# Moving mask clears, counts and first list steps in a sparse two-layer graph attention kernel

## The chip, the core and the metric

The kernel runs on one core of a Trainium2 chip, as one program and one launch. The metric is the device time in microseconds from the start to the end of the program: three runs of the kernel before gave 1828.33, 1829.27 and 1834.35 us, so its median is 1829.27 us.

The engines are named as the profile names them: PE is TensorE's matmul, PEld its weight load, DVE is VectorE, ACT is ScalarE, POOL is GpSimd, SP is SyncE, which here only issues DMAs.

## The reference

Two graph attention layers over 3327 nodes with 1024 features, each with a residual and a layer norm. The adjacency is 0 or 1, symmetric, with some 16 neighbours per node and its diagonal set. Layer 0 has 8 heads of 128, layer 1 has one head of 1024.

```python
# layer 0
h = (x @ W).reshape(C, H, D)
alpha_src = einsum('hcd,hd->hc', h_heads, a_src)
alpha_dst = einsum('hcd,hd->hc', h_heads, a_dst)
e = alpha_src[:, :, None] + alpha_dst[:, None, :]
e = where(e >= 0, e, 0.2 * e)
e = where(adj[None] == 0, -inf, e)
out = einsum('hij,hjd->hid', softmax(e), h_heads)
x = layernorm(x + out)
# layer 1: h = x @ W; the same with one head, a relu, a residual and a layer norm
```

## The kernel before

Nodes are cut into NT = 26 tiles of 128 (P). The kernel has two stages. The first one, "projection with list work", projects each tile of x with the weights of layer 0, stores the rows of h in device memory, and beside it turns each tile's dense adjacency rows (a mask of 128 x 3328 bytes) into lists of neighbours. The second stage, `sparse`, gathers the listed rows of h with indirect DMAs, weighs and sums them, and does layer 1 in the same manner. A third part, `by_pairs`, is for dense graphs and isn't entered with this input. The change touches only the first stage.

In that stage nothing is scheduled by the compiler: `manual_schedule` (L510) keeps the order in which the Python code issues instructions, on every engine. Each engine runs its own instructions in that order and waits with semaphores for what the others make.

The projection of a tile t has three column cuts c of 347, 347 and 346 columns. `flip(t, g)` (L533) transposes half of x's tile on PE into the one PSUM bank "T" and copies it out on ACT (L199). `project(t, c)` (L538) does the eight matmuls over k into one of two banks "A". `keep(t, c)` (L549) copies the result out on ACT (L561); for c = 2 it also copies the scores (L556) and makes `factors`, small exponentials on ACT and four small instructions on POOL (L329 to L333). After the third cut the rows go out with a DMA on SP (L564).

The list work of a tile has these steps:

- `words` (L335): POOL clears the tile's own diagonal block in the mask with an affine_select (L342); ACT passes twice over the mask to count each row's neighbours in two halves (L346, into `junk`) and makes `deg_b` (L348); DVE folds eight mask bytes into one word (L353, `wd`, three instructions). `count(t)` (L566) calls it and then issues the load of the mask two tiles ahead on POOL's DMA queue (`load_mask`, L524). There are three mask buffers.
- `ends` (L359): a tiny PE matmul of `deg_b` with a triangle (L362) makes running sums over the rows; ACT copies them (L367) and 13 small POOL instructions make places of them (L369 to L382).
- `ends2` (L384): the same for what overflows: PE (L387), ACT (L388), six POOL instructions (L389 to L395).
- `keys` and `columns` (L397, L406), two calls each: DVE picks each row's largest words, then its columns (L308, L310).
- `ways` (L421), three ACT instructions; `places` (L431), DVE (L435 to L441); `spread` (L443), four ACT instructions (L447, `mvg`).
- `give` (L451), five times: PE matmuls that move the lists to their places (L459, L466). `take` (L470): ACT copies the result (L478 to L485) and SP stores a part. `sources` (L488): DVE makes the indices of the gathers (L493 to L507).

The generator `listing` (L572) puts these into rounds. Round t has, in order: four steps with `give` of tile t and `keys` or `columns` of tile t+1, with `ends(t+3)` in the second and `ends2(t+3)` in the fourth; one step with the last two `give`, `take(t)`, `ways(t+1)` and `count(t+4)`; one with `sources(t)`; one with `places(t+1)`; one with `spread(t+1)`. That is eight steps; round -1 has no tile t and is shorter.

`pace` (L608) advances the generator: it is called after every second k of a paced `project`, and keeps the number of steps done at a share of the paces so far. `slots` holds the paces counted and the paces in all; `done` the steps done.

Before the main loop (L854) the first tiles are issued by hand (L779 to L853): `count(0)`, two steps of the generator, cuts of tiles 2 and 0, `ends` of tile 0, `count(1)`, two more steps, and so on, as the diff shows. In the main loop iteration t projects cuts 0 and 1 of tile t and cut 2 of tile t+1 and flips tile t+2. From t = 13 (NTH) on, `sums_so_far` (L617) joins: it gathers rows of h that are already stored (L629, POOL), makes weights (DVE, L637 to L650) and sums them on PE (L659); each pace advances it by one step as well.

Of the kernel before, what the change touches and what calls it, by code (L numbers as in the profile page):

```python
# [14 lines left out]
OP = mybir.AluOpType  # L15
# [4 lines left out]
P = 128  # L20
# [6 lines left out]
def kernel(  # L27
# [28 lines left out]
    nc = tc.nc  # L56
    N, D = x.shape
    H, DH = a0_src.shape
    NT = (N + P - 1) // P
# [254 lines left out]
    class Edges:  # L314
# [10 lines left out]
        def factors(self):  # L325
# [6 lines left out]
            nc.gpsimd.tensor_copy(mv[:, 1, :], r[:, 1, :])  # L332
            nc.gpsimd.tensor_tensor(mv[:, 2, :], r[:, 1, :], mv[:, 1, :], OP.subtract)  # L333

        def words(self, ad, junk):  # L335

            sbuf, ph, t = self.ph.sbuf, self.ph, self.t  # L340
            own = ad[:, t * P : (t + 1) * P].bitcast(mybir.dt.int8)
            nc.gpsimd.affine_select(  # L342
                out=own, in_=own, pattern=[[1, P]], compare_op=OP.not_equal, fill=0.0, base=0, channel_multiplier=-1
            )
            for n in range(2):
                nc.scalar.activation(junk, ad[:, n * THR : (n + 1) * THR], AF.Copy, accum_out=self.d[:, n : n + 1])  # L346
            self.deg_b = sbuf("deg_b", [P, 2], 4, dt=BF16)
            nc.scalar.activation(self.deg_b, self.d, AF.Copy)  # L348
            w = ad.bitcast(I32)
            for n in range(3):  # L350
                m = WD >> n
                half = sbuf(f"wd{n}", [P, m], 4 if n == 2 else 1, dt=I32)
                nc.vector.scalar_tensor_tensor(  # L353
                    half, w[:, m:], 1 << n, w[:, :m], op0=OP.logical_shift_left, op1=OP.bitwise_or
                )
                w = half
            self.bytes = w.bitcast(U8)
# [152 lines left out]
    with ExitStack() as own, tc.manual_schedule():  # L510
        ph = Phase(own, "proj", {"A": 2, "T": 1})
# [4 lines left out]
        xts, xT, ads, hts, accs = {}, {}, {}, {}, {}  # L516
        lists = [Edges(ph, t) for t in range(NT)]

        def load_x(t):
            if t < NT:  # L520
                xts[t] = ph.sbuf("x", [P, D], 2)
                load_rows(xts[t], x, t)
# [10 lines left out]
        def flip(t, g, who=None):  # L533
            if g == 0:
                xT[t] = ph.sbuf("xT", [P, KT, P], 2) if t else part.sbuf("z", [P, KT, P], 1, "xT")
            (who or ph).turned(xT[t], xts[t] if g == 0 else xts.pop(t), g)

        def project(t, c, paced=True, between=None):  # L538

            acc = accs[t, c] = bank("A", [P, CUTS0[c + 1] - CUTS0[c]], "mm")  # L540
            for k in range(KT):
                nc.tensor.matmul(  # L542
                    acc, xT[t][:, k, :], wt[:, k, CUTS0[c] : CUTS0[c + 1]], start=k == 0, stop=k == KT - 1
                )
                if k == 3 and between:
                    between()
                if paced and k % 2 == 1:
                    pace()

        def keep(t, c):  # L550
            if t not in hts:
                hts[t] = ph.sbuf("ht", [P, HW0], 3)
            ht, acc, c0 = hts[t], accs.pop((t, c)), CUTS0[c]
            m = min(CUTS0[c + 1], D) - c0
            if c == 2:
                nc.scalar.activation(sd0[:, t].rearrange("p a h -> p (a h)"), acc[:, m:], AF.Copy)  # L556
                lists[t].factors()
                nc.scalar.activation(ht[:, D : D + H], acc[:, m + H :], AF.Exp)
                nc.scalar.activation(ht[:, D + H :], acc[:, m + H :], AF.Exp, scale=SLOPE)
                scored.add(t)  # L560
            nc.scalar.activation(ht[:, c0 : c0 + m], acc[:, :m], AF.Copy)  # L561
            kept[t] = kept.get(t, 0) + 1
            if kept[t] == 3:
                nc.sync.dma_start(h0_d[t * P : (t + 1) * P, :HW0], hts.pop(t))  # L564

        def count(t):  # L566
            if t < NT:
                lists[t].words(ads.pop(t), junk)
                if t:
                    load_mask(t + 2)  # L570

        def listing():  # L572

            for t in range(-1, NT):
                old, new = lists[t] if t >= 0 else None, lists[t + 1] if t + 1 < NT else None
                for s in range(4):
                    if old and s:
                        old.give(s - 1)
                    if new:
                        (new.keys, new.columns)[s // 2](s % 2)  # L580
                    if s == 1 and 2 < t + 3 < NT:
                        lists[t + 3].ends(tri_b)
                    if s == 3 and 2 < t + 3 < NT:
                        lists[t + 3].ends2(all_b)
                    yield
                if old:
                    old.give(EB - 1)
                    old.give(EB)
                    old.take()
                if new:  # L590
                    new.ways()
                count(t + 4)
                yield
                if old:
                    old.sources()
                    yield
                while new and t + 1 not in scored:
                    yield
                if new:
                    new.places()  # L600
                    yield
                    new.spread()
                    yield

        scored, kept, soon = set(), {}, []
        steps, slots, done = listing(), [0, 0], [0]

        def pace():  # L608
# [202 lines left out]
        for g in range(NG):  # L811
            nc.vector.memset(tri[g * GT : (g + 1) * GT, g * GT : (g + 1) * GT], 1.0)
        nc.gpsimd.affine_select(
            out=tri, in_=tri, pattern=[[1, P]], compare_op=OP.is_ge, fill=0.0, base=0, channel_multiplier=-1
# [8 lines left out]
        )  # L823
        all_b = pool.tile([P, P], BF16, bufs=1, name="all_b")
        nc.vector.tensor_copy(all_b, tri)
        count(0)
        for _ in range(2):
            next(steps)
# [8 lines left out]
        project(1, 2, False)  # L837
        keep(1, 2)
        lists[0].ends2(all_b)
        lists[1].ends(tri_b)  # L840
        flip(3, 0)
        load_x(5)
        count(2)

        done[0], slots[:] = 4, [9, (NT - 3) * 12 + 13]
        project(2, 2, True, lambda: flip(3, 1))
        keep(2, 2)
        flip(4, 0)
        lists[1].ends2(all_b)
        lists[2].ends(tri_b)  # L850
        project(3, 2, True, lambda: flip(4, 1))
        keep(3, 2)
        lists[2].ends2(all_b)  # L853
        for t in range(3, NT):  # L854
            load_x(t + 3)
            if 4 <= t < 4 + KT:
                nc.sync.dma_start(wt1[:, t - 4, :], w1[(t - 4) * P : (t - 3) * P, :])
            if t == 12:
                n, own_a = NT - 1, pool.tile([P, NT], I32, bufs=1, name="own")
                nc.vector.memset(own_a[:, n:], 0)  # L860
                step, m = adj.ap[0][0] + 1, rows(n)
                nc.sync.dma_start(
                    own_a[:, :n], bass.AP(tensor=adj.tensor, offset=adj.offset, ap=[[step, P], [P * step, n]])
                )
                nc.sync.dma_start(
                    own_a[:m, n:], bass.AP(tensor=adj.tensor, offset=adj.offset + n * P * step, ap=[[step, m], [1, 1]])
                )
            if t == 11:
                ph.iota([P, P], [[1, P]], "io_t", base=1, dst=io_t)
                same = ident[: NG * H, : NG * H].rearrange("p (g h) -> p g h", g=NG)  # L870
                met = meets.rearrange("p (g t) -> p g t", g=NG)
                nc.vector.tensor_reduce(met[:, :, 0], same, AX.X, OP.max)
                nc.vector.tensor_copy(met[:, :, 1:], met[:, :, :1].to_broadcast([NG * H, NG, GT - 1]))
                nc.vector.tensor_reduce(heads, same.rearrange("p g h -> p h g"), AX.X, OP.max)
            if t == 16:
                nc.gpsimd.tensor_copy(loop, own_a)
            if t in (9, 10):
                table, w = (h0_d, HW0) if t == 9 else (y_d, HW)
                blank = pool.tile([P, 1, HP - w], F32, bufs=1, name=f"blank{t}")
                nc.gpsimd.memset(blank, 0.0)  # L880
                nc.sync.dma_start(
                    table[:, w:].rearrange("(t p) w -> p t w", p=P), blank.to_broadcast([P, NT, HP - w])
                )
            if t == NTH:
                soon.append(sums_so_far())
            for c in (0, 1):
                project(t, c)
                keep(t, c)
            if t + 2 < NT:
                flip(t + 2, 0)  # L890
            if t + 1 < NT:
                project(t + 1, 2)
                keep(t + 1, 2)
            if t + 2 < NT:
                flip(t + 2, 1)
# [624 lines left out]
```

## Time and profile before

One execution was profiled. It took 1945.79 us, with a span of 1944.1 us from the first to the last instruction; the three timed runs lie at 1828.33 to 1834.35 us.

| what | value |
|---|---|
| median of the timed runs | 1829.27 us |
| profiled execution | 1945.79 us |
| its span | 1944.1 us |
| PE busy | 1633.7 us, 84% |
| DVE busy | 1184.5 us, 61% |
| POOL busy | 1092.2 us, 56% |
| ACT busy | 573.4 us, 29% |
| one clear of a mask block (L342, POOL, x26) | 294 ns |
| one count pass (L346, ACT, x52) | 1591 ns |
| first fold of words (L353, DVE, x26) | 591 ns |
| DVE waiting for the clear (L353 <- L342), 0 to 600 us | 57.0 us, 13 times |
| ACT waiting for the clear (L346 <- L342), 0 to 600 us | 14.8 us, 5 times |

The busy shares are means over both stages. The first stage ends near 570 us of the span; what happens there has to be read from that stretch. A matmul's busy time in the profile is modelled, since matmuls overlap. In the profile's lines the number after the name of an engine is the line of the kernel; "<-" names what ended a wait.

### The profile page before, as it was taken

What the parts mean: (1) busy time and instruction counts of PE and PEld (TensorE: products, weight loads), DVE (VectorE), ACT (ScalarE), POOL (GpSimd) and SP (SyncE); (2) the same over time, 40 slices, a digit from 0 to 9 for tenths busy, and PEclk for the clock granted to TensorE, in tenths of its full rate; (3) what the DMA queues carried; (4) which work ended last, traced back from release to release, by engine and by line L of the source; (5) the groups of instructions that cost most, each with busy time, mean ns of one, the idle gap of its engine ahead of it and who ended that gap; (6) DMA issues with size and microseconds to landing.
All of it is one profiled execution on the core that took longest, in us unless ns stands there. A gap on an engine that the chain in (4) does not pass through costs nothing.

```text
span 1944.1 us, 35431 instructions
## 1 busy us (share of the span) xinstructions
PE 1633.7 (84%) x13168; PEld 919.9 (47%) x13168; DVE 1184.5 (61%) x3261; ACT 573.4 (29%) x1565; POOL 1092.2 (56%) x1580
## 2 busy tenths in 40 slices
PE   8699989989994777777777665798989999899988
PEld 5466556655563554554455442243434434333433
DVE  6699988777765776777777774243444344434342
ACT  5656554444321222222222121022122221222121
POOL 4433346656555666666666555565656666565640
PEclk9899999999996878888878877899999999999999
DMA  6555779887779999999999998899999999899980
GB/s 178 91 130 114 144 152 293 255 249 238 247 271 349 381 391 393 383 393 371 402 386 386 374 313 301 310 374 340 346 350 369 335 394 342 331 362 340 325 302 33
DMA packets 183364, 585.16 MB, mean 301 GB/s; under 512 B 36168, under 2 KB 42824, under 8 KB 183182
## 3 DMA queue, kind: packets, MB, share of 16 engines
q0 software_dynamic: 131056, 457.74, 68.4%
q1 hardware_dynamic: 52126, 125.06, 17.2%
q8 instruction: 107, 1.75, 0.4%
q14 instruction: 75, 0.61, 0.1%
HBM read 586.09 MB, written 51.22 MB: 328 GB/s over the span
## 4 chain that ended last, share of the span: by engine, by line
PE 43%; issue 10%; DVE 6%; ACT 4%; DMA 4%; POOL 1%; another core or an unknown queue 0%; DVEq 0%; ACTq 0%; POOLq 0%
PE mm L1267 17%; PE acc L1235 13%; PE acc L1129 8%; PE acc L1110 2%; DMA src<-h_d,idx 2%; PE tr L196 1%; ACT L1193 1%; PE acc L1118 1%; DVE e L1098 1%; ACT own L1076 1%; DMA near<-h_d,idx 1%; DVE pr L982 1%; DVE st L217 1%; ACT L220 1%; DMA src<-y_d,idx 1%
## 5 line engine op out<-in xcount | busy, mean ns | idle before, releaser
L542 PE MATMUL mm<-wt,xT 128*128 128x347 f32 (+1 forms) x1248 | 416.6, 475 | 6.8 <-ACT ht L561 3.3
L1267 PE MATMUL mm<-wt,xT 128*128 128x512 f32 x832 | 395.5, 613 | 2.6 <-issue 2.3
L1017 POOL DMA_INDIRECT src<-y_d,idx x248 | 249.1, 1005 | 166.8 <-PE acc L1235 71.0
L542 PEld LDWEIGHTS mm<-wt,xT 128*128 128x128 f32 x1248 | 228.5, 195 | 118.3 <-issue 19.7
L1017 POOL DMA_INDIRECT src<-h_d,idx x184 | 196.5, 1068 | 121.3 <-PE acc L1129 35.8
L1267 PEld LDWEIGHTS mm<-wt,xT 128*128 128x128 f32 x832 | 152.3, 193 | 211.5 <-issue 206.7
L1270 DVE SCALAR_TENSOR_TENSOR o<-mm,y 128x512 f32<-128x512 f32 x52 | 36.0, 692 | 322.2 <-PE acc L1235 126.4
L1017 POOL DMA_INDIRECT near<-y_d,idx x168 | 169.5, 1009 | 108.7 <-PE acc L1235 48.3
L1129 PE MATMUL acc<-src,e 128*32 128x128 f32 x2944 | 161.3, 324 | 52.1 <-issue 47.5
L1017 POOL DMA_INDIRECT near<-h_d,idx x120 | 130.6, 1088 | 82.4 <-PE acc L1129 31.0
L1235 PE MATMUL acc<-src,es 128*32 128x341 f32 x1488 | 130.6, 485 | 41.8 <-DVE es L1226 31.8
L1129 PEld LDWEIGHTS acc<-src,e 128*32 128x32 f32 x2944 | 111.5, 130 | 113.4 <-issue 93.8
L1098 DVE TENSOR_TENSOR e<-oh,way 128x1024 f32<-128x1024 f32 x104 | 127.1, 1222 | 59.3 <-ACT w L1096 43.1
L1129 PE MATMUL acc<-near,e 128*32 128x128 f32 x2048 | 116.0, 333 | 48.7 <-issue 34.8
L199 ACT ACTIVATE xT<-tr 128x512 f32<-128x512 f32 x104 | 62.1, 598 | 299.9 <-PE tr L196 151.6
L1129 PEld LDWEIGHTS acc<-near,e 128*32 128x32 f32 x2048 | 79.7, 133 | 93.7 <-issue 84.4
L1096 ACT ACTIVATE w<-way 128x32 f32<-128x32 f32 x104 | 20.3, 195 | 351.4 <-DVE way L1094 186.6
L1249 ACT ACTIVATE z<-y,ri 128x342 f32<-128x342 f32 (+1 forms) x78 | 39.5, 569 | 277.0 <-issue 121.6
L1235 PE MATMUL acc<-near,es 128*32 128x342 f32 (+1 forms) x1008 | 85.8, 469 | 21.3 <-DVE es L1226 14.0
L629 POOL DMA_INDIRECT near<-h_d,idx x76 | 82.1, 1080 | 31.5 <-issue 22.9
L1235 PEld LDWEIGHTS acc<-src,es 128*32 128x32 f32 x1488 | 44.4, 114 | 115.0 <-issue 61.1
L346 ACT ACTIVATE junk<-ad 128x1664 uint8<-128x1664 uint8 x52 | 83.8, 1611 | 16.2 <-POOL ad L342 14.8
(242 smaller groups left out, 2587.8 us busy)
## 6 DMA issues: line engine op xcount, KB each, us to landing
h_d<-ht SPq DMA_DIRECT2D x26, 520.0 KB
own<-h_d SPq DMA_DIRECT2D x26, 520.0 KB
y_d<-y SPq DMA_DIRECT2D x26, 514.0 KB
y<-y_d SPq DMA_DIRECT2D x26, 514.0 KB
x<-in_x_dram SPq DMA_DIRECT2D x25, 512.0 KB
y<-in_x_dram SPq DMA_DIRECT2D x25, 512.0 KB
out_dram<-o SPq DMA_DIRECT2D x25, 512.0 KB
ad<-in_adj_dram POOLq DMA_DIRECT2D x25, 415.9 KB
```

The lines of the kernel that those rows point to most:

```text
L199: nc.scalar.activation(part, tr, AF.Copy)
L346: nc.scalar.activation(junk, ad[:, n * THR : (n + 1) * THR], AF.Copy, accum_out=self.d[:, n : n + 1])
L542: nc.tensor.matmul(acc, xT[t][:, k, :], wt[:, k, CUTS0[c] : CUTS0[c + 1]], start=k == 0, stop=k == KT - 1)
L629: nc.gpsimd.indirect_dma_start(out=src[n % 3][:, g, :], out_offset=None, in_=h0_d[:THR, :], in_offset=bass.IndirectOffsetOnAxis(ap=idx[:, ...
L1017: nc.gpsimd.indirect_dma_start(out=s[:, g, :w], out_offset=None, in_=table[:n, :], in_offset=bass.IndirectOffsetOnAxis(ap=idx[:, t, b * NG ...
L1098: nc.vector.tensor_tensor(e, oh.unsqueeze(2).to_broadcast([P, ng, H, wide]), wp.unsqueeze(3).to_broadcast([P, ng, H, wide]), OP.mult,)
L1110: nc.tensor.matmul(self.acc[j - 1].rearrange("p h d -> p (h d)"), ident, self.h[:, (j - 1) * HALF : j * HALF], start=False, stop=False,)
L1129: nc.tensor.matmul(self.acc[h // 4][g * GT : (g + 1) * GT, h % 4, :], e[:, g, h, :], rowsof[:, g, h, :], start=first and h % 4 == 0, stop= ...
L1235: nc.tensor.matmul(self.acc[c][to, :m], es[:, g, :], s[:, g, CUTS[c] : CUTS[c + 1]], start=b == 0, stop=b == EB,)
L1249: nc.scalar.activation(z[:, cut], self.res[:, cut], AF.Copy, scale=ri[:, 1:2])
L1267: nc.tensor.matmul(acc, xT[:, k, :], wt1[:, k, half], start=k == 0, stop=k == KT - 1)
L1270: nc.vector.scalar_tensor_tensor(o[:, half], acc, 0.0, res[:, half], op0=OP.max, op1=OP.add)
```

## The change

Three things are changed, all in the order of issue. The number of instructions and of DMAs stays the same.

1. `words` loses its clear; a new function `clear` has it. The first three masks are cleared in one go before `count(0)`. In round t the mask of tile t+4 is cleared in the third step (s == 2); `count` clears a mask that hasn't been cleared yet, which is so for tile 3 only.
2. In a round `count(t + 4)` stands last, in a step of its own, behind `spread(t + 1)`; `places` and `spread` share a step. A round still has eight steps, the last one seven instead of six.
3. The first rounds: the slots start at 4 of 284 instead of 9 of 289, so the first pace no longer runs four steps at once; `ends` and `ends2` of tiles 1 and 2 are put between other cuts and flips; cut 0 of tile 3 is projected before `ends2` of tile 2 and left out of the loop's first iteration.

```diff
+        def clear(self, ad):
+            own = ad[:, self.t * P : (self.t + 1) * P].bitcast(mybir.dt.int8)
             nc.gpsimd.affine_select(
                 out=own, in_=own, pattern=[[1, P]], compare_op=OP.not_equal, fill=0.0, base=0, channel_multiplier=-1
             )
+
+        def words(self, ad, junk):
+            sbuf = self.ph.sbuf
             for n in range(2):
                 nc.scalar.activation(junk, ad[:, n * THR : (n + 1) * THR], AF.Copy, accum_out=self.d[:, n : n + 1])
...
+        def clear(t):
+            if t < NT and t not in cleared:
+                cleared.add(t)
+                lists[t].clear(ads[t])
+
         def count(t):
             if t < NT:
+                clear(t)
                 lists[t].words(ads.pop(t), junk)
                 if t:
                     load_mask(t + 2)
...
                     if s == 1 and 2 < t + 3 < NT:
                         lists[t + 3].ends(tri_b)
+                    if s == 2 and t >= 0:
+                        clear(t + 4)
                     if s == 3 and 2 < t + 3 < NT:
                         lists[t + 3].ends2(all_b)
                     yield
...
                 if new:
                     new.ways()
-                count(t + 4)
                 yield
                 if old:
                     old.sources()
...
                 if new:
                     new.places()
-                    yield
                     new.spread()
                     yield
+                count(t + 4)
+                yield
...
+        for t in range(3):
+            clear(t)
         count(0)
...
         lists[0].ends2(all_b)
-        lists[1].ends(tri_b)
         flip(3, 0)
         load_x(5)
+        lists[1].ends(tri_b)
         count(2)
 
-        done[0], slots[:] = 4, [9, (NT - 3) * 12 + 13]
+        done[0], slots[:] = 4, [4, (NT - 3) * 12 + 8]
         project(2, 2, True, lambda: flip(3, 1))
         keep(2, 2)
+        lists[1].ends2(all_b)
         flip(4, 0)
-        lists[1].ends2(all_b)
-        lists[2].ends(tri_b)
         project(3, 2, True, lambda: flip(4, 1))
         keep(3, 2)
+        lists[2].ends(tri_b)
+        project(3, 0)
+        keep(3, 0)
         lists[2].ends2(all_b)
...
-            for c in (0, 1):
+            for c in (0, 1)[t == 3 :]:
                 project(t, c)
                 keep(t, c)
```

More of the change, by code (lines that the diff above doesn't have):

```diff
@@ L333, in factors @@
             nc.gpsimd.tensor_tensor(mv[:, 2, :], r[:, 1, :], mv[:, 1, :], OP.subtract)
-        def words(self, ad, junk):
-            sbuf, ph, t = self.ph.sbuf, self.ph, self.t
-            own = ad[:, t * P : (t + 1) * P].bitcast(mybir.dt.int8)
+        def clear(self, ad):
+            own = ad[:, self.t * P : (self.t + 1) * P].bitcast(mybir.dt.int8)
             nc.gpsimd.affine_select(
@@ L600, in listing @@
                     new.places()
-                    yield
                     new.spread()
                     yield
-        scored, kept, soon = set(), {}, []
+                count(t + 4)
+                yield
+        scored, cleared, kept, soon = set(), set(), {}, []
         steps, slots, done = listing(), [0, 0], [0]
```

## The prediction

> **What bounds the kernel now.** I read the page's slices first, for the stages. The projection with the list work, all that the change touches, lies in the first twelve of 40 slices (48.6 us each). After it DMA is at 9 and granted TensorE clock at 6 to 8.
>
> ```profile
> span 1944.1 us, 35431 instructions
> ...
> PE   8699989989994777777777665798989999899988
> ...
> DVE  6699988777765776777777774243444344434342
> ...
> PEclk9899999999996878888878877899999999999999
> DMA  6555779887779999999999998899999999899980
> ```
>
> The chain of waits reaches back only to 595 us, so for the projection I read the busy times by stretch (PE, PEld, DVE, ACT and POOL busy, clock, DMA share, GB/s).
>
> ```profile
> 50.00:100.00 50.00, 35.27 (x142) 22.99 (x141) 32.37 (x91) 28.70 (x80) 23.26 (x112) 0.86 0.51 89
> 100.00:150.00 50.00, 48.19 (x227) 31.84 (x227) 47.11 (x137) 31.56 (x106) 18.92 (x85) 1.00 0.58 126
> 150.00:200.00 50.00, 48.23 (x218) 31.67 (x218) 47.18 (x135) 32.82 (x99) 16.24 (x76) 1.00 0.63 136
> ...
> 400.00:450.00 50.00, 42.43 (x385) 27.20 (x378) 36.10 (x99) 21.42 (x66) 27.86 (x60) 0.93 0.86 250
> ```
>
> Three regimes: a start with holes; 95 to 265 us with PE and VectorE both at 95%; then, from tile 13 on, PE loaded and VectorE with slack. Next the waits in 45 to 95 us (total, times, longest), then VectorE's in 265 to 570 us:
>
> ```profile
> DVE wd L353 <- POOL ad L342: 14.6, 3, 6.2
> ...
> PE xp L466 <- ACT mvg L447: 9.3, 1, 9.3
> PE dd L362 <- ACT cnt L388: 5.4, 2, 4.5
> ```
>
> ```profile
> DVE wd L353 <- POOL ad L342: 42.4, 10, 6.9
> DVE kq L493 <- ACT xs L480: 14.0, 3, 5.5
> ```
>
> From 95 to 265 us VectorE waits once, 1.6 us, for another cause: it sets the pace there, and the timeline gives a round of 15.2 us. In it, keys take 5.2 us (125.99 to 131.19), columns 4.9 (to 136.05), words 1.2 (to 137.25), sources 2.9 (122.08 to 124.95), places 1.0 (to 125.99). At the start the timeline shows the knot:
>
> ```profile
> 59.62 1.59 ACT L346 ACTIVATE junk<-ad 128x1664 uint8<-128x1664 uint8 x1 [3.77 <-POOL ad L342]
> 59.62 0.59 DVE L353 SCALAR_TENSOR_TENSOR wd<-ad 128x416 int32<-128x416 int32 x1 [4.96 <-POOL ad L342]
> ...
> 64.14 0.16 PE L362 MATMUL dd<-deg_b,tri_b 128*128 128x2 bf16 x1 [4.52 <-ACT cnt L388]
> ...
> 78.66 0.48 PE L466 MATMUL xp<-mvg,place 128*128 128x168 bf16 x3 [9.34 <-ACT mvg L447]
> ```
>
> A 0.29 us clear waits behind ends' 13 small POOL instructions (56.35 to 59.3); ScalarE and VectorE stop behind it. Then four steps fall on the first pace, two counts and ways lie ahead of the spread on ScalarE, and PE stands 9.3 us.
>
> **What the Trainium skill says.** "PSUM — Partial Sum Buffer", section Engine vs sequencer instructions: ScalarE, VectorE and GpSimd are strict FIFO, and matmuls start in program order. The trace agrees: the transposes of 64.24 run only after the L362 that waited 4.52 us. "TensorE: Matmul & The Clock Gate", What's actually happening: an idle window of about 3.4 us halves the clock. Here the start has a granted mean of 0.77 in 60 to 90 us. "Perfetto Trace Analysis", Identifying the Most-Contended Engine, warns that matmul busy time is a poor measure; so I use rates: 16 matmul records in 4.82 us, 0.29 each.
>
> **The change part by part.** All against the profiled 1945.8 us; the median, 1829.3, differs in the stage after 600 us (clock 0.72 to 0.89 there), so I subtract the same microseconds from it.
>
> *Clears.* Same 26 instructions of 0.29 us, moved on POOL. None lengthens a chain: POOL is busy 16 of 50 us. A clear now waits for its mask, and ends2, factors and gathers are queued behind it. In rounds the mask is issued a round and three steps earlier, some 20 us; a mask is 415.9 KB, at the 107 GB/s of 90 to 120 us 4 us. For mask 3 it is some 8 us. I take 0; the other end is 3 us, once.
>
> *Start.* Followed by hand with the trace's durations. Count 1 starts on ScalarE at 55.8 (after L367) instead of 59.6 and ends at 59.5; VectorE's words at 54.7, columns done at 60.8. L388 at 60.7, then ends 1 on PE at 61.0 (was 64.14). Count 2 to 65.2, words 2 by 62. Ways at 65.8 to 67.2, places to 67.5, spread to 68.5; clear 3 about 67; count 3 on ScalarE 68.5 to 72.2, words 3 on VectorE to 68.9. Project 2,2 is done at 66.4 without the 9.3 us hole. But keep 2,2 and the copy of flip 4,0 are behind count 3 (about 74.6), and flip 4,1 needs the single T bank: PE, there at 69.8, stands 4.9 us. Project 3,0 begins near 78.3 (was 90.37). VectorE starts keys of tile 1 at 68.9 (was 74.2), ends columns at 78.8, then waits for the take at 83 (project 3,0, third pace); sources, places, words: keys of tile 2 at 88.6, before 95.6. That is -7.0 us on VectorE, the engine that sets the pace next. If the 4.9 us stall goes, -11; if it doubles, -2.
>
> *Pace.* 216/289 steps a pace become 216/284. Tile 13 begins at slot 137, step 102.4 before; now at slot 132, step 100.4. Two steps of eight in a 15.2 us round fall after tile 13, where VectorE has slack: -3.8 us. PE would allow it: per tile 48 records of 0.29 and two groups of transposes of 0.6, 15.1 us, times 8/9.13, plus 1.5 of give and ends, 14.7 a round (before 15.0).
>
> *Counts last, tiles 4 to 12.* VectorE's sum doesn't change; words only swap places with sources and places. But ends of tile t+4 now waits for a count that stands two steps ahead of it, behind the spread on ScalarE. From the start of places, P: mvs done P+0.4; spread 1.28, to P+1.7; the two junk passes and deg_b 3.7 (119.64 to 123.32), P+5.4; L362 on PE P+5.6; to the last give 5.7 (127.22 to 132.95), P+11.3; take up to L480 0.8, P+12.1. VectorE comes to sources at P+1.0+1.2+5.2+4.9=P+12.3. So the new wait is hidden by 0.2 us only. The cover is gone when another ScalarE instruction gets in between: per tile two copies of 0.46, a group of 0.87, two of 0.6, 3.0 us; 0.88 tiles a round, a quarter of the steps lie in that stretch: 0.66 us on average, less 0.2, some 0.45 a round, for 9.7 rounds: +4.4 us. Behind the waiting L362 on PE are all matmuls, and keys' successors need their take. Bounds: 0, if these copies fall elsewhere or the spread goes earlier by as much (it no longer has junk ahead of it); +2 a round, +20, if all of them lie there.
>
> *From tile 13 on.* The 42.4 us of VectorE are mostly not to be had: at 460.53 words begins, and take is far enough for sources at 459.6 only, so sources would wait until then. What goes is words' 1.2 us and the rest of the POOL chain between take and sources. PE has gaps that end with VectorE's late marks, weights and places: 1.3, 2.3, 4.8, 1.7, 0.5 and 1.0 us (before L659 and L466, 289 to 492 us). At most 1.3 each: -6.7; I take -5. The two steps more in this stage cost PE 0.3. New waits for deg_b: at 441.81 mvs is done, deg_b would come at 447.1, and L362 stands at 449.54: hidden by 2.4 us. Bounds: -12 (also POOL's share of the wait) and +6 (each such round 1 us late).
>
> *Order of ends and flips before the loop, SP.* x loads move by a few instructions; they are issued some 20 us before use: 0.
>
> Sum: -7.0 - 3.8 + 4.4 - 5 = -11.4; 1945.8 becomes 1934.4, the median 1829.3 becomes 1818.
>
> **Rivals.** (a) *Deeper gain*: no ScalarE copy gets in between, and the later stage gains 12: -10.8-12 = -23, 1806. For it: the spread is freed from the junk ahead of it. Against: the chain's slack of 0.2 us. (b) *No change*: the wait at L362 costs 0.7 a round (+7) and the later gaps stay: -3.8, 1825.5. For it: PE and VectorE are so balanced that any new wait shows. (c) *Slower*: deg_b behind the spread becomes the loop that sets every round, at 2 us over 15.2 for 9.7 rounds (+19), and 1 us in each of six later rounds (+6): -10.8+25 = +14, 1843. It decides above 1.1 us a round, where the 10.8 is eaten. For it: three loops of 15 us; against: spread starts earlier than before in rounds like 249 to 265 us, where it was 1.2 us late behind deg_b and copies. (d) The clears come before their masks: +3 in all, no case of its own.
>
> **How the numbers follow.** Likeliest, with rounds at 15.2 to 15.8 us: 0.45, 1812 to 1823. (a) 0.15, (b) 0.20, (c) 0.20. A measurement of this kernel can tell 0.3%, 5.5 us, from none. Faster: 0.45 less a little plus 0.15: 0.58; same 0.22, slower 0.20. The range takes (a) whole, down to 1803, (b) whole and the milder part of (c): up to 1836.
>
> **What would show it.** Right: no waits of words for the clear; PE's 9.3 us at L466 gone and a stall of some 5 us before flip 4,1; keys of tile 2 near 88 us; rounds of 15.2 to 15.8; last projection matmul near 560 instead of 570.5. Wrong: waits PE dd L362 <- ACT deg_b of over 1 us in most rounds, rounds of 16.5 or more; POOL waiting for a mask; or a start no earlier than 95 us.

## The result, and the profile after

The kernel after takes 1802.24 us (1801.29 to 1802.86, four runs) where the kernel before, beside it, took 1830.01 (1828.33 to 1834.35): a ratio of 0.9848, 95% interval 0.9831 to 0.9864. The forecast was 1818, with a range down to 1803: the sign is right, the gain of 27.8 us is more than twice the 11.4 forecast, and the time lies 0.8 us below the range.

The runs here fall into groups in which the kernel before takes 1830, 1930, 1965 or 1970 us; so every kernel is compared only with runs of the kernel before made beside it. The profile shown ahead of the prediction was one of the long ones (1945.79 us). Below, "before" is a profile of the same kernel at 1830.33 us (run e0c), the level of the profile of after (1802.57 us). The page of after, its slices of 45 us:

```profile
span 1800.9 us, 35423 instructions
...
PE   8899989999995676666776765599999999999998
...
DVE  6799899898765887877777787334444444444443
PEclk9999999999996887888768668799999999999999
DMA  7565869999879999999999999899999999999980
```

PE has no slice below 8 left in the projection; DMA stands at 9 from the seventh slice to the tenth. After the last projection matmul the two kernels take the same, 1265.4 us before and 1266.8 after. The whole gain lies in the first stage, whose last projection matmul moves from 563.2 to 534.1 us. The same stretches as before, by the busy times of each engine (PE, PEld, DVE, ACT, POOL, clock, DMA share, GB/s), and the waits of the start, for after:

```profile
50.00:100.00 50.00, 44.45 (x192) 29.14 (x191) 38.58 (x109) 31.23 (x98) 28.23 (x123) 0.97 0.65 124
100.00:150.00 50.00, 46.24 (x207) 30.78 (x206) 45.42 (x133) 30.11 (x96) 15.30 (x71) 0.97 0.48 108
...
400.00:450.00 50.00, 48.65 (x444) 32.59 (x443) 44.59 (x122) 24.26 (x76) 37.90 (x83) 1.00 0.93 280
```

```profile
PE tr L196 <- ACT xT L199: 5.0, 1, 5.0
PE dd L365 <- ACT cnt L391: 0.5, 1, 0.5
...
DVE wd L356 <- POOL ad L338: 2.2, 1, 2.2
```

In the start PE's 9.3 us wait for the spread is gone, a stall of 5.0 us at the single bank T is there (forecast 4.9), and words' wait for the clear fell from 14.6 to 2.2 us. From 100 to 150 us the engines are *less* busy than before (PE 46.2 for 48.2), and in 400 to 450 us much more (48.7 for 42.4). That is the pattern to explain: a gain at the start, a little lost in the middle, most of it won after tile 13.

Three marks divide the stage. "Start" is from the first keys of tile 0 to those of tile 2, "middle" from there to the start of tile 13's projection (its cut 2, which is projected first), "later" from there to the start of the last projection matmul.

| us | start | middle | later | last projection matmul |
|---|---|---|---|---|
| before | 46.1 | 161.0 | 306.0 | 563.2 |
| after | 39.4 | 163.3 | 283.6 | 534.1 |
| measured change | -6.7 | +2.3 | -22.4 | -29.1 |
| forecast | -7.0 | +0.6 (pace -3.8, counts +4.4) | -5 | -11.4 |

The missing 2.3 us of -29.1 is the preamble before the first keys: it takes 47.5 to 51.4 us from profile to profile, also of one kernel. So one term of the sum is far off: *From tile 13 on*. What PE waited for there, in before and then in after (total, times, longest):

```profile
PE part L659 <- DVE mvs L435: 12.6, 4, 4.8
PE part L659 <- DVE e L650: 4.1, 3, 1.9
PE xp L466 <- ACT mvg L447: 3.8, 2, 2.3
PE tr L196 <- ACT xT L199: 3.3, 2, 1.7
PE dd L387 <- POOL more_b L375: 2.0, 3, 1.4
```

```profile
PE dd L365 <- ACT deg_b L351: 2.9, 3, 1.5
PE dd L390 <- POOL more_b L378: 2.4, 2, 1.3
PE dd L390 <- DVE met L706: 1.7, 1, 1.7
...
PE part L670 <- DVE mvs L438: 0.8, 1, 0.8
```

Before, PE stood for what VectorE makes late: the weights `e` of the sums (L650), and the spread of what places make (`mvg`). The four waits that the profile puts down to `mvs` fit `e` better: L659 reads `e`, and in each of them VectorE had made `e` just before `mvs`. The longest, in before:

```profile
406.53 0.59 DVE L353 SCALAR_TENSOR_TENSOR wd<-ad 128x416 int32<-128x416 int32 x1 [4.68 <-POOL ad L342]
...
408.08 0.18 DVE L493 TENSOR_TENSOR kq<-io_k,xs 128x16 f32<-128x16 f32 x1
...
411.58 1.23 DVE L650 TENSOR_TENSOR e<-oh,w 128x1024 f32<-128x1024 f32 x1
...
413.06 1.27 PE L659 MATMUL part<-far,e 128*32 128x128 f32 x28 [4.80 <-DVE mvs L435]
```

Words waits for the clear, sources come behind words, `e` behind sources, and PE stands 4.80 us for `e`. The other three (3.05, 2.15 and 2.56 us) follow in the same order on waits of words of 6.39, 6.42 and 5.75 us. After, 0.8 us of the `mvs` waits is left. The whole stretch, before and after:

```profile
257.00:563.00 306.00, 278.35 (x2480) 183.05 (x2479) 236.22 (x649) 136.68 (x435) 185.92 (x390) 0.98 0.81 249
```

```profile
250.00:534.00 284.00, 275.11 (x2497) 183.23 (x2495) 238.46 (x656) 137.98 (x436) 197.56 (x403) 0.99 0.88 270
```

PE is idle 27.7 of 306 us before and 8.9 of 284 after: 18.8 of the 22 us. The other 3.2 us is PE's busy time, 278.35 and 275.11. It would fit a clock of 0.99 for 0.98 (278.35 x 0.98 / 0.99 = 275.5), but at 0.99, too, PE is busy 284.4 us of that stage in a longer run of after (e4), so this isn't shown. Where VectorE lost the time, one round of before shows best, that of tile 15 (start, duration, engine, line; the wait in brackets):

```profile
338.48 0.20 ACT L480 ACTIVATE xs<-xp 128x8 f32<-128x8 f32 x1
...
339.85 1.11 POOL L629 DMA_INDIRECT near<-h_d,idx  x1 [0.53 <-issue]
...
343.88 0.99 POOL L629 DMA_INDIRECT near<-h_d,idx  x1 [0.30 <-issue]
344.89 0.30 POOL L342 TENSOR_SCALAR_AFFINE_SELECT ad<-ad 128x128 int8<-128x128 int8 x1
...
345.22 0.59 DVE L353 SCALAR_TENSOR_TENSOR wd<-ad 128x416 int32<-128x416 int32 x1 [5.66 <-POOL ad L342]
...
346.45 0.18 DVE L493 TENSOR_TENSOR kq<-io_k,xs 128x16 f32<-128x16 f32 x1
```

What sources need was there at 338.7 (L480). But words stands ahead of sources on VectorE, words needs the clear, and the clear stands on POOL behind four gathers, which start 1.3 to 1.4 us apart. "Perfetto Trace Analysis" of the Trainium skill, section DMA Instruction — SWDGE (GPSIMD), says that a gather's slice on POOL is the writing of its descriptors, not the move of its data. The trace fits: each holds POOL about 1 us, and the clear starts as the fourth slice ends. VectorE stands 5.66 us, and sources begin 7.8 us after L480 ended, 1.2 of it words. The other long waits have the same cause: in the seven of over 3 us POOL ran two to four gathers, 1.2 to 4.1 us of its time, and in six of them also the six small instructions of `ends2`, 1.1 us, before it came to the clear.

I measured this lag (end of L480 to start of L493) for rounds 12 to 21. Before it is 5.6, 2.1, 4.4, 7.8, 2.8, 2.6, 4.2, 4.9, 4.0 and 4.5 us, 42.9 in all. After it is 4.2 in all, and never over 2.2. In the last rounds, which have no count, it is 0.0 in before as well.

### The profile page after: what moved, and what is told of

The parts are those of the page before. It is cut to its first block, busy times and chain, and to the rows that moved or that the text cites. A ratio compares the mean times of both kernels' runs of the same rounds, so it can differ in the third digit from the quotient of the medians.

```text
span 1800.9 us, 35423 instructions
## 1 busy us (share of the span) xinstructions
PE 1540.2 (86%) x13168; PEld 906.1 (50%) x13168; DVE 1187.6 (66%) x3261; ACT 574.3 (32%) x1565; POOL 1112.8 (62%) x1580
## 4 chain that ended last, share of the span: by engine, by line
PE 41%; DMA 13%; DVE 8%; issue 4%; ACT 1%; POOL 1%; DVEq 0%; ACTq 0%; POOLq 0%
PE mm L1282 21%; PE acc L1250 13%; DMA src<-h_d,idx 8%; PE acc L1144 3%; DMA near<-h_d,idx 3%; PE acc L1125 2%; DVE e L1113 2%; PE tr L196 1%; DVE own L1087 1%; DVE pr L1183 1%; DVE pr L997 1%; DMA end<-h_d,idx 1%; POOL src L1032 1%; DMA av<-in_L_gnn_a_dram 1%; PE acc L1133 0%
## 5 line engine op out<-in xcount | busy, mean ns | idle before, releaser
L545 PE MATMUL mm<-wt,xT 128*128 128x347 f32 (+1 forms) x1248 | 410.0, 470 | 3.1 <-DMA wt<-in_L_gnn_W_dram 3.1
L1282 PE MATMUL mm<-wt,xT 128*128 128x512 f32 x832 | 388.3, 605 | 0.0
L545 PEld LDWEIGHTS mm<-wt,xT 128*128 128x128 f32 x1248 | 226.3, 192 | 120.5 <-issue 24.1
L1282 PEld LDWEIGHTS mm<-wt,xT 128*128 128x128 f32 x832 | 150.0, 190 | 199.5 <-issue 194.5
L1144 PE MATMUL acc<-src,e 128*32 128x128 f32 x2944 | 126.5, 343 | 42.9 <-DVE e L1113 23.4
L1250 PE MATMUL acc<-src,es 128*32 128x341 f32 x1488 | 124.5, 469 | 10.3 <-issue 9.1
L1144 PE MATMUL acc<-near,e 128*32 128x128 f32 x2048 | 85.3, 336 | 38.1 <-DVE e L1113 21.8
L1144 PEld LDWEIGHTS acc<-near,e 128*32 128x32 f32 x2048 | 73.2, 137 | 62.8 <-issue 41.0
L640 POOL DMA_INDIRECT near<-h_d,idx x76 | 82.8, 1089 | 26.7 <-issue 18.8
L1167 PE MATMUL den<-heads,met 32*128 32x8 f32 x52 | 13.7, 335 | 93.5 <-DVE met L1166 93.5
```

Of the source, the lines that this page charges most:

```text
L545: nc.tensor.matmul(acc, xT[t][:, k, :], wt[:, k, CUTS0[c] : CUTS0[c + 1]], start=k == 0, stop=k == KT - 1)
L640: nc.gpsimd.indirect_dma_start(out=src[n % 3][:, g, :], out_offset=None, in_=h0_d[:THR, :], in_offset=bass.IndirectOffsetOnAxis(ap=idx[:, ...
L1144: nc.tensor.matmul(self.acc[h // 4][g * GT : (g + 1) * GT, h % 4, :], e[:, g, h, :], rowsof[:, g, h, :], start=first and h % 4 == 0, stop= ...
L1250: nc.tensor.matmul(self.acc[c][to, :m], es[:, g, :], s[:, g, CUTS[c] : CUTS[c + 1]], start=b == 0, stop=b == EB,)
L1282: nc.tensor.matmul(acc, xT[:, k, :], wt1[:, k, half], start=k == 0, stop=k == KT - 1)
```

## The experiments

The two theories: the later gain comes from the place of the counts, since words no longer stand ahead of sources (T1), or from the early clear, since words no longer wait for POOL (T2). The table has every run of a changed kernel; "first" means the new first rounds, "counts" the counts last, "clear" the early clears.

| run | has | median us (runs) | before | ratio, 95% interval | start | middle | later |
|---|---|---|---|---|---|---|---|
| e0 | before again | 1960.2 (1) | 1965.4 | | 45.9 | 161.0 | 317.5 |
| e1 | counts, first | 1954.9 (20) | 1965.4 | 0.996, 0.9939 to 0.9982 | 44.8 | 164.5 | 320.5 |
| e2 | clear, first | 1930.4 (4) | 1965.4 | 0.9829, 0.9748 to 0.991 | 39.4 | 158.5 | 303.7 |
| e3 | clear, counts | 1958.7 (20) | 1965.4 | 0.9971, 0.9946 to 0.9995 | 38.9 | 164.9 | 312.7 |
| e0b | before again | 1935.9 (1) | 1930.2 | | 47.0 | 161.0 | 312.1 |
| e4 | after again | 1903.7 (6) | 1930.2 | 0.9847, 0.9796 to 0.9898 | 39.9 | 163.3 | 302.1 |
| e5 | clear | 1899.4 (4) | 1930.2 | 0.9807, 0.9757 to 0.9858 | 37.3 | 161.2 | 297.4 |
| e6 | first | 1916.0 (12) | 1930.2 | 0.9919, 0.9885 to 0.9953 | 47.7 | 158.1 | 317.6 |
| e0c | before again | 1830.3 (1) | 1831.9 | | 46.1 | 161.0 | 306.0 |
| e7 | clear from tile 16 on | 1809.8 (4) | 1831.9 | 0.9883, 0.9866 to 0.9899 | 45.1 | 161.1 | 287.9 |
| e8 | after, ends later | 1792.5 (4) | 1831.9 | 0.9783, 0.9761 to 0.9805 | 40.0 | 157.9 | 279.9 |
| e9 | clear, first (as e2) | 1800.0 (4) | 1831.9 | 0.9828, 0.9811 to 0.9845 | 39.1 | 158.8 | 289.4 |
| e10 | counts | 1961.6 (13) | 1969.6 | 0.9966, 0.9941 to 0.9992 | 44.6 | 167.1 | 321.2 |
| e11 | first (as e6) | 1948.6 (4) | 1969.6 | 0.9877, 0.9846 to 0.9908 | 47.2 | 158.3 | 321.4 |
| e12 | clear, counts (as e3) | 1947.4 (4) | 1969.6 | 0.9884, 0.9853 to 0.9914 | 39.6 | 166.7 | 311.2 |

### One part of the change taken back: e1, e2, e3, with e0 beside them

e1 clears in `count` again:

```diff
-                    if s == 2 and t >= 0:
-                        clear(t + 4)
...
-        for t in range(3):
-            clear(t)
```

> The changed kernel with the clears back inside count (directly ahead of the count's passes); counts last and the new first rounds stay. Theory T1 (my prediction's reading: the gain of the later stage is mainly that words and the clear's wait no longer stand between take and sources, so the place of count carries it): the clear behind a count that is last is short of cover only at the start, so at most 8 us are lost: 1802 to 1810 us. Theory T2 (the early clear itself carries the gain, because VectorE's 42 us of waits on the clear return wherever count stands): 1815 us or more, with waits of wd for the clear in ten or more rounds.

e2 puts the counts back in the step of `ways`, and gives places and spread a step each again:

```diff
                 if new:
                     new.ways()
+                count(t + 4)
                 yield
...
-                count(t + 4)
-                yield
```

> The changed kernel with count back in the step of take and ways (places and spread again in steps of their own); early clears and new first rounds stay. T1: the gain of the later stage (some 15 us) goes, the start's stays: 1812 to 1820 us. T2: nearly all of the gain stays, and the 11.6 us of PE waiting for deg_b in the first rounds go as well: 1795 to 1804 us.

e3 has the first rounds of the kernel before (slots [9, ...], the order of ends and flips, cut 0 of tile 3 in the loop):

```diff
-        done[0], slots[:] = 4, [4, (NT - 3) * 12 + 8]
+        done[0], slots[:] = 4, [9, (NT - 3) * 12 + 13]
...
-        project(3, 0)
-        keep(3, 0)
...
-            for c in (0, 1)[t == 3 :]:
+            for c in (0, 1):
```

> The changed kernel with the first rounds as before (slots 9 of 289, ends and ends2 of tiles 1 and 2 and cut 0 of tile 3 where they were); early clears and counts last stay. T1 as predicted: the start is worth 7 us of VectorE and 3.8 us of pace, so 1809 to 1815 us. T2 (the early clear alone untangles the start): 1802 to 1805 us, with PE's wait at the first give under 3 us.

The kernel before once more, for a profile of the same level:

> The kernel before once more, for a profile whose own time lies near the timed runs. Expected 1828 to 1835 us. T1 and T2: the first stage ends near 571 us of the span as in the first profile, since that profile's extra 116 us lie after 600 us; then the second stage takes some 1258 us, 8 us less than the changed kernel's 1266, so part of the first stage's 36 us is given back. A rival (T3: the first profile was slow in the first stage too): last projection matmul near 562 us, and nothing is given back.

Without the early clear (e1) start and later stage are near those of before (44.8 and 320.5; e0 45.9 and 317.5), and with it, without the counts last (e2), both are short (39.4 and 303.7): T2. T2's other sign for e1 failed: words waits for the clear in three later rounds (8.1 us) and not in ten; 19.4 us more of its waits stand for no cause that the profile shows. The counts last cost the middle: 164.5 and 164.9 with them, 158.5 without. Taking the first rounds back (e3) leaves the start at 38.9, so the gain there isn't theirs.

The time of e3 fits neither theory: 0.9971 would be some 1825 us where before takes 1830. Its later stage, 312.7 us, is only 4.8 shorter than e0's, although its lag is 0.3 us in the ten rounds together; VectorE waits 54.0 us there for the take. So a short lag is not enough for a short later stage. e0 missed its expected time, too: before took 1960 us here, not 1830. Next, single parts were added to the kernel before.

### One part alone: e5, e6, and after again

e5 is before with `clear` in the third step and the first three clears, nothing else:

```diff
+                    if s == 2 and t >= 0:
+                        clear(t + 4)
...
+        for t in range(3):
+            clear(t)
         count(0)
```

> The kernel before with the early clears alone: counts beside ways, first rounds as before. T6 (early clear and new first rounds each carry their own share): the start keeps PE's 9.3 us at the first give, VectorE's 42 us of waits on the clear become some 20 us of waits on the take, and 8 to 14 us are gained, 0.993 to 0.996. T7 (the two only work together): under 4 us, 0.998 or more.

e6 is before with the new first rounds only, the reverse of e3's edit:

```diff
-        done[0], slots[:] = 4, [9, (NT - 3) * 12 + 13]
+        done[0], slots[:] = 4, [4, (NT - 3) * 12 + 8]
...
+        project(3, 0)
+        keep(3, 0)
```

> The kernel before with the new first rounds alone: clears inside words, counts beside ways. T6: PE's 9.3 us at the first give are gone and tile 13 begins 5 to 8 us earlier; the later stage is as before; 5 to 10 us gained, 0.995 to 0.997. T7: the clear behind ends' POOL chain still holds ScalarE and VectorE at the start, so under 4 us, 0.998 or more.

Beside them ran the kernels after and before, unchanged:

> The changed kernel again, beside single parts of the change and the kernel before on one chip[...]. Expected: 0.984 of the kernel before where before takes 1830 us; on a chip where before takes some 1960 us, T4 (the gain is of matmuls and waits and is the same in microseconds) says 27 us, 0.986; T5 (the gain shrinks where PE's stalls that the profile calls issue fill the later stage, as in the runs without one part) says 10 us or less, 0.995.

> The kernel before, for a profile on the same chip as e4 to e6. Where it takes some 1830 us: last projection matmul near 561 us (1829 less the changed kernel's 1267 us after its own), tile 13 at 258 us. Where it takes some 1960 us: 571 us, as in the two profiles so far.

The clear alone brings as much as the whole change: 0.9807 and 0.9847, with intervals that overlap. Both theories had put it lower. It takes the start from 47.0 to 37.3 us and the later stage from 312.1 to 297.4. PE still stands 9.4 us at the first give in e5, and in e6, where that wait is gone, the start is no shorter (47.7): PE's 9.3 us weren't what made the start long. The first rounds alone take 2.9 us from the middle, by the pace. e6 as a whole, 0.9919, gains more than T6 and T7 say.

In these longer groups the time and the first stage don't move together: after (e4) is 26.5 us faster than before, as T4 says, but its last projection matmul comes only 11.0 us earlier. In the group of e7 to e9 they do, to within 4 us (e7 22.1 and 21.5, e9 31.9 and 28.2, e8 39.4 and 37.0). So sizes are read from that group, and the others tell directions.

### Only the later rounds: e7

Whether the later gain follows from the start, or is the clear's own there, is told apart by before with the clear moved in rounds 12 and later only:

```diff
+                    if s == 2 and t >= NTH - 1:
+                        clear(t + 4)
```

> The kernel before with one edit: in rounds 12 and later (from tile 13's projection on) the clear stands in the third step; all earlier clears stay inside words. T8 (the later stage runs in a loop take, words, sources, places, give, in which the clear waits on POOL behind gathers and ends2, so that sources begins 2 to 8 us after take in each round): the start and the rounds up to tile 13 as before (tile 13 at 208 us after the first keys), sources begins 0 to 0.5 us after take in rounds 12 to 21, and the later stage is 12 to 17 us shorter: 0.991 to 0.994. Rival T9 (the later stage is shorter only because the earlier one lets the list work start ahead): no change, 0.999 to 1.001, although the waits on the clear are gone.

And before once more, the profile used above:

> The kernel before, for a profile on the chip of e7 to e9. If that chip takes 1830 us for it, last projection matmul near 561 us; else 568 to 573 us.

Start and middle stay as before (45.1, 161.1), and the later stage falls by 18.1 us, the time by 22.1; T9 falls. So that gain is its own, made by moving ten instructions of 0.29 us. One round of e7:

```profile
331.31 0.29 POOL L338 TENSOR_SCALAR_AFFINE_SELECT ad<-ad 128x128 int8<-128x128 int8 x1
...
332.20 0.57 DVE L356 SCALAR_TENSOR_TENSOR wd<-ad 128x416 int32<-128x416 int32 x1
...
333.86 0.19 DVE L496 TENSOR_TENSOR kq<-io_k,xs 128x16 f32<-128x16 f32 x1 [0.35 <-ACT xs L483]
...
335.84 1.11 POOL L640 DMA_INDIRECT near<-h_d,idx  x1 [0.15 <-issue]
```

The clear is done before the gathers, words runs without a wait, and sources wait only 0.35 us for their own data (L483, the L480 of before). Words still stands ahead of sources here; its place is not what mattered. The lag is 0.0 or 0.1 us in seven of the rounds 12 to 21 and 2.3 to 2.7 in three, 7.9 in all for 42.9 before, so T8 holds in the main. That the clear must be out from behind the gathers and `ends2` on POOL is the part of T2 shown.

### The counts: e9, e10, e12, e11

e9 and e12 are e2 and e3 again, beside other runs of before; e11 is e6 again; e10 is before with only the counts last, each with its clear, and places and spread in one step:

```diff
                 if new:
                     new.ways()
-                count(t + 4)
                 yield
...
+                count(t + 4)
+                yield
```

> The changed kernel with count back beside ways, again (early clears and new first rounds stay): the version that the runs so far point to, with the first stage 8 us shorter than the changed kernel's. Expected 0.980 of the kernel before, where the changed kernel took 0.985; if counts last costs nothing in the end, 0.985.

> The kernel before with counts last alone: clears inside words, first rounds as before. T12 (with counts last, words no longer stand between take and sources, so the clear's wait is off that loop as well, and the later stage gains without the early clear): sources within 0.5 us of take, later stage 290 us instead of 306; the start as before, first rounds 5 us longer for PE's wait for deg_b; 0.993 to 0.996. T13 (the clear, now behind a count that is last, holds deg_b and the words of the next keys instead, so the early clear is needed): later stage 300 us or more, 0.998 to 1.003.

> The changed kernel with the first rounds as before, again: 0.997 in e3, where its later stage was 29 us longer than the changed kernel's on another chip. T14: the early clear untangles the start here too (keys of tile 2 at 39 us after the first), and the first stage is within 6 us of the changed kernel's: 0.985 to 0.988. T15: 0.995 or more.

> The kernel before with the new first rounds alone, again: in e6 the time was 0.992 of the kernel before although its first stage ended no earlier. If the first stage tells (T14): 0.999 to 1.003. If the new first rounds act on what comes after the first stage (T15): 0.990 to 0.994 with a second stage of 1255 us or less instead of 1265.

The counts last cost the middle 4.5 us with the new first rounds (163.3 in after, 158.8 in e9), and 3.7 to 5.5 (e3 and e12 less e5) with the old. The wait is the one that the prediction named; in 95 to 250 us of after:

```profile
PE dd L365 <- ACT deg_b L351: 11.6, 8, 3.1
```

e9 has none of it. In the later stage after is 5.8 us faster than e9 (283.6, 289.4). In e9 words still waits 13.1 us for the clear there, in after not at all, but that is one profile each, and e5, without the counts last, has a shorter later stage than after again (297.4, 302.1). Over the whole kernel the two give 0.9848 and 0.9828 with overlapping intervals: beside the early clear and the new first rounds the place of the counts makes no difference that these runs can tell. With the old first rounds it seems to: e3 and e12 have 0.9971 and 0.9884 and later stages of 312.7 and 311.2 us, e5, without the counts last, 0.9807 and 297.4. e12 missed what T14 said of its first stage, too: 568.0 us to its last projection matmul. Why the counts last cost there is open.

e10 tells why the place of the counts alone isn't enough. VectorE's waits in it, 258 to 570 us:

```profile
DVE wd L356 <- POOL ad L338: 24.5, 5, 11.9
DVE kq L496 <- ACT xs L483: 22.5, 8, 5.9
```

Sources now start within 1.7 us of the take in every round. But words meets the late clear behind them, and the next round's keys wait instead: the later stage stays at 321.2, as T13 says. The wait moved, it didn't go. T1 falls.

The pairs of one kernel don't all agree: e2 and e9 do (0.9829, 0.9828), and e6 and e11 just overlap (0.9919, 0.9877), but e3 and e12 are apart (0.9971, 0.9884). Differences under 1% between groups are therefore not read. e9 stayed short of the 0.980 that was expected. e11, at 0.9877, gains more than T15 says, but not by the second stage of 1255 us that T15 named: 1376.2 us follow its last projection matmul.

### What remains: ends one step later, e8

After's middle still has the 11.6 us of L365. e8 is after with `ends(t + 3)` behind the clear in the third step, and `ends2(t + 3)` in the step of sources:

```diff
-                    if s == 1 and 2 < t + 3 < NT:
-                        lists[t + 3].ends(tri_b)
                     if s == 2 and t >= 0:
                         clear(t + 4)
-                    if s == 3 and 2 < t + 3 < NT:
-                        lists[t + 3].ends2(all_b)
+                    if s == 2 and 2 < t + 3 < NT:
+                        lists[t + 3].ends(tri_b)
...
                     old.sources()
+                    if 2 < t + 3 < NT:
+                        lists[t + 3].ends2(all_b)
```

> The changed kernel with ends of tile t+3 one step later (in the third step, behind the clear) and ends2 in the step of sources. T10 (counts last costs through PE's wait for deg_b at ends, 11.6 us in the first rounds): the wait is gone, rounds before tile 13 are 15.2 us again, and tile 13 begins 4 to 5 us earlier than in the changed kernel, 198 us after the first keys: 0.982 of the kernel before. Rival T11 (PE stands there anyway, since VectorE sets the pace): the waits move to the first give or to the copies and tile 13 begins within 1 us of the changed kernel's 203 us.

In 90 to 250 us of e8:

```profile
PE dd L365 <- ACT deg_b L351: 7.1, 5, 2.6
```

The middle goes to 157.9 (-5.4), the later stage to 279.9, where PE is idle 5.7 of 280 us. T10 is right on the marks (tile 13 begins 197.9 us after the first keys), but the wait is only cut from 11.6 to 7.1 us, so it isn't shown that all of the 5.4 us come from it. At 1792.47 us and 0.9783 this beats both kernels: its interval ends at 0.9805, that of after begins at 0.9831.

## Why the prediction was right in sign and wrong in size

*Clears.* Priced at 0, at worst 3 us once: POOL waited for a mask once at the start, 1.2 us. The price of the move was right. What the late clear had cost was counted under *Start* and *From tile 13 on*.

*Start.* -7.0 forecast, -6.7 measured; keys of tile 2 at 88.6 forecast, at 87.2 measured; the stall at bank T 4.9 and 5.0. The following by hand held. But it took clears and first rounds as one edit; e5 and e6 show that the clear carries it alone (37.3 us with the old first rounds, 38.9 and 39.6 in e3 and e12), whether or not PE stands at the first give.

*Pace.* -3.8 forecast. The kernels with the new first rounds and without counts last have middles of 158.1 to 158.8, for 161.0: -2.2 to -2.9.

*Counts last, tiles 4 to 12.* +4.4 forecast, +4.5 measured. The agreement is luck in part: L365 waits 1.45 us on average in eight rounds, where 0.45 in 9.7 was reckoned. That sums to 11.6 us, of which only 4.5 show in the middle; where the rest was taken up isn't shown.

*From tile 13 on*: the step that failed, a term of the right mechanism and sign. -5 was taken, from bounds of -12 and +6; it measured -22.4. The sentence was that VectorE's 42.4 us "are mostly not to be had", since take would hold sources at 459.6 when words began at 460.53. That was one round, taken for all ten. Its wait was long, 6.09 us, but its take came late, so that most of the wait lay ahead of the take and the lag was only 2.2 us. In the same profile the ten lags sum to 33.1 us and reach 7.8, some 12 us of them words itself. From the one round each gap of PE was capped at 1.3 us, though the gaps listed beside it were up to 4.8. And the list was short: its six gaps sum to 11.6 us, about the bound of -12, while PE was idle 27.1 of that stage's 312.5 us. So the bound "also POOL's share" had the right cause and still too small a size. Of the -22.4 us, e7 shows 18.1 to be the clear's own; the other 4.3 aren't told apart.

As I read it, the path is a loop: take, words (waiting for the clear), sources, places and weights on VectorE, then PE's sums and give, then the next take. That VectorE is idle 23% of that stage doesn't mean that a wait in this loop is free; PE's own work bounds what its removal can bring. PE's idle time there was 27.7 us, so -22.4 is most of what could be had.

*The base.* The prediction took its profile to differ from the timed runs only after 600 us, and named the clock there. At the level of 1830 us the first stage of before already ends earlier, at 563.2 instead of 570.5 us, and the mean granted clock is lower, not higher (0.906, 0.918 in the long profile). The gain was subtracted in microseconds, and PE's idle time in the later stage is nearly the same in both (27.1 and 27.7 us), so this cost the forecast little.

*Rivals.* (a), a deeper gain at 1806, is nearest in time, but not as it was told: the ScalarE copies did get in between (of 0.44 us ahead of the deg_b wait at 105.8 us, of 0.43 and 0.58 ahead of that at 200.2). (b), no change, and (c), slower by deg_b, fail: L365 in the later stage waits 2.9 us in all. In the middle two rounds took 17.2 and 17.6 us, each with a wait of 2.1 us for deg_b, but the eleven rounds have a mean of 15.8 (before 15.4), not the 16.5 or more that was named as the sign.

## What to carry to other kernels

When a small instruction sits on a queue with DMA issues, price the queue ahead of it, not its duration; 0.29 us of clear held VectorE up to 6.4 us. Before saying that a wait "isn't to be had" because another ends at the same time, read that in every round and take the sum, and check it against the idle time of the engine that sets the pace. After moving a wait's consumer, look where the wait goes next: here it came back behind sources until its producer was moved.

## What was not expected of the hardware, and what stays open

The same kernel takes 1830 to 1970 us in different groups. Part lies in the first stage, too: in the longer groups PE's weight loads of the sums stand more often for no cause that the profile shows. In the later stage of the same kernel, e4 and then after:

```profile
PEld part L670 <- issue: 30.8, 54, 3.3
```

```profile
PEld part L670 <- issue: 12.8, 23, 1.3
```

The stage takes 302.1 and 283.6 us, so these 18.0 us are about the size of the difference. In e3 and e12 the line is longest, 42.0 and 39.6 us. What PE waits for there isn't shown; no run was made for it. Long and short runs move the same 585 MB, but after the first stage at 343 GB/s in e0 (DMA share 0.92) and at 376 in before at 1830 us (0.97); whether that is cause or effect isn't shown.

The new first rounds alone (e6, e11) shorten the kernel by 0.8 and 1.2%, though their first stage isn't shorter (574.6 us, e0b 567.7). In the profiles of e6 and e0b layer 1, from its first gather to the end, took 746.1 and 773.7 us, and 741.7 in that of after (e4). Nothing in the change touches that layer, and at the level of 1830 us the span after the last projection matmul is 1263.5 to 1266.8 us for all kernels. The cause stays open.
